# Part of an attention kernel's row maxima taken from one key half and a rectified key difference

## Chip, core and metric

The kernel runs on one core of a Trainium2 chip. The metric is the time of one execution on the device, in microseconds. PE is the matrix engine, DVE the vector engine, ACT the scalar engine, POOL the GpSimd engine, and SP the queue that issues the DMAs.

## The reference

`x` has 8 batches of 1024 tokens of 256 features. One transformer layer, with grouped-query attention and a feed-forward part with ternary weights:

```
h = layernorm(x)
q, k, v = h @ Wq, h @ Wk, h @ Wv          # 16 query heads, 4 key heads, head size 16
q, k = rope(q), rope(k)
p = softmax(q k^T / sqrt(256))            # over the 1024 keys of the batch
x = x + layernorm((p v) @ Wo)
x = x + layernorm(layernorm(x) @ ternary(W)^T * alpha + bias)
```

Everything is float32. Before the exponentials the kernel subtracts each query's largest score, so it computes all scores twice: once with queries on the partitions, to find the maxima, and once with keys on the partitions, for the exponentials and the product with v.

## The kernel before

A *unit* is half a batch, 512 tokens; there are 16. A unit has four *blocks* (one query head of each key head), a block has 8 *steps* (one tile of 128 keys each), so a unit has 32 steps (`SPU`) and the kernel 512. A step has four score tiles of 128 keys by 512 queries.

Queries and keys are stacked in `q_st` and `k_st` as 64 rows a head: the parts high, low, high of q against high, high, low of k (float32 split in two), and two rows that carry the split negative maximum against rows of -1. Two heads share the 128 rows. `q_st` has two buffers (a unit each), `k_st` and `v_aug` (v with a column of ones) have three (a batch each).

The work of PE, DVE and ACT is in the program's order, written by `window()`. A window has three of a block's 32 exp tiles (two in its last). For each, `exp_one` issues one score matmul (L628) into one of three PSUM buffers of one bank and ACT's exponential (L643); behind each, `max_scores` issues one maxima matmul (L576): 128 queries against 512 keys. Two of them (the index `v`, `part = v % 2`) fill a tile `sm` of two banks, with two buffers, and DVE reduces its 1024 columns to one (L590). Then come parts of other stages (`parts_of_step`), and at the end `av_piece` (L663), the product of the exponentials of two windows earlier with v. Maxima run 48 tiles (12 steps) ahead of the exps. When a block's 16 tiles of maxima are done, `shift_split` (L603) splits them, and `shift_rows` transposes them (L610), copies them on ACT (L612) and sends them into `q_st` by two DMAs (L619).

The other stages are put at steps by tables. `P_PARTS` holds a unit's `Project` (layer norm, q, k, v), starting four units' steps early, relative to `SPU * (u - 4)`; `T_PARTS` holds its `Tail` (scaling, Wo, layer norms, feed-forward). For a unit from the third on: `kv_and_dram` makes k and v transposed and sends k to DRAM and back as `k_rot`; `kt` rotates it, splits it (L157, L162) and stores the parts to DRAM (`dk`, L430), and `stack_keys` loads them into `k_st` (L481); `v` transposes v into `v_aug` (L366, L372); `q` and `q_to_dram` (L472) and later `stack_queries` (L542) do the same for q. In the main part POOL's and SP's orders are chosen by a planner with simulated costs. The first units get their keys on the chip (`PickRows`), and the last unit has a tail of its own (`LastTail`), which uses free buffers of `k_st` and `v_aug`.

Of the kernel before, what the change touches and what calls it, by code (L numbers as in the profile page):

```python
# [16 lines left out]
P = 128  # L17
# [3 lines left out]
HD = 16  # L21
UT = 4
UQ = UT * P
EPS = 1e-5
THRESH_FACTOR = 0.7


@with_exitstack
def kernel(
# [103 lines left out]
    k_st, v_aug, q_st = [], [], []  # L133
    for i in range(2):
        q_st.append(const.tile([P, G, 2, UQ], F32R, name=f"q_st{i}"))
    for i in range(3):
        k_st.append(const.tile([P, 2, S], F32R, name=f"k_st{i}"))
        v_aug.append(const.tile([P, NK, HKV, 32], F32, name=f"v_aug{i}"))

# [10 lines left out]
    def fill_constant_parts(i):  # L150
        if i > 0:
            fill_rows(k_st[i], 1, NROW, 64 - NROW)
        nc.gpsimd.memset(v_aug[i], 1.0)

    def split_hi(eng, hi, src):
# [149 lines left out]
    class Project:  # L305
# [54 lines left out]
        def v(self):  # L360

            lo = 0 if self.u < 2 else DK
            pt = psum([P, UT, P], f"ptv_{self.u}")
            for t in range(UT):
                src = self.kv_t[lo:, t * P : (t + 1) * P]
                nc.tensor.transpose(pt[:, t, lo:], src, ident[lo:, lo:])  # L366
            if lo == 0:
                self.k_rot = qkp.tile([P, UT, DK], F32, tag="k_rot", name=f"k_rot_{self.u}")
                nc.scalar.copy(self.k_rot, pt[:, :, :DK])
            if self.u == 0:  # L370
                self.split_q(0, (0,))
            nc.scalar.copy(  # L372
                v_aug[self.b % 3][:, self.half * UT : (self.half + 1) * UT, :, 0:HD],
                pt[:, :, DK:].rearrange("p t (r d) -> p t r d", d=HD),
            )

# [30 lines left out]
        def kv_and_dram(self):  # L407

            u = self.u
            for p in range(2):  # L410
                self.kv(p)
            d_k = dram.tile([DK, UQ], F32, tag="d_k", name=f"d_k_{u}")
            nc.sync.dma_start(out=d_k, in_=self.kv_t[:DK])
            self.k_rot = qkp.tile([P, 2, P], F32, tag="k_rot", name=f"k_rot_{u}")
            src = d_k.rearrange("(m e) (g t) -> e g m t", e=2, t=P)
            for e in range(2):
                nc.sync.dma_start(out=self.k_rot[:, e, :], in_=src[e])

        def kt(self):
            rotate(  # L420
                self.eng, self.k_rot, cos_kt_sb[:, self.half], sin_kt_sb[:, self.half],
                work.tile([P, 2, P], F32, tag="t2k", name=f"t2k_{self.u}", bufs=1),
            )
            hl = qkp.tile([P, 2, 2, P], F32R, tag="k_parts", name=f"ks_{self.u}")
            split(self.eng, hl[:, 0], hl[:, 1], self.k_rot)
            dk = self.dk = dram.tile([2, DK, UQ], F32, tag="dk", name=f"dk_{self.u}")
            dst = dk.rearrange("l (m e) (g t) -> l e g m t", e=2, t=P)
            for l in range(2):
                for e in range(2):
                    nc.sync.dma_start(out=dst[l, e], in_=hl[:, l, e, :].bitcast(F32))  # L430
            self.stack_keys()

        def q_product(self, p):
            if self.q_rot is None:
# [36 lines left out]
                    src = self.hl["q"][64 * c : 64 * (c + 1), l].rearrange("p e t -> p (e t)")  # L471
                    nc.sync.dma_start(out=rows[l, c], in_=src.bitcast(F32))  # L472

        def stack_keys(self):

            keys = slice(self.half * UQ, (self.half + 1) * UQ)
            src = self.dk.rearrange("l (r a d) t -> a l d r t", a=2, d=HD)
            for a in range(2):
                for band, l in enumerate((0, 0, 1)):
                    row = 64 * a + HD * band  # L480
                    nc.sync.dma_start(  # L481
                        out=k_st[self.b % 3][row : row + HD, :, keys].bitcast(F32), in_=src[a, l]
                    )

    def row_pickers():

# [68 lines left out]
            return q_st[u % 2][:, j, r2, :]  # L555
        return q_st[u % 2][:, :, r2, j * P : (j + 1) * P]

    def max_scores(v):


        i, k = divmod(v // 2, 2 * NK)
        u, part = i // G, v % 2
        if i == 0:
            a, ch, t, r2 = 1 - part, k // NK, k // 2 % UT, k % 2
        else:
            a, ch, t, r2 = 1 - k % 2, part, k // 4, k // 2 % 2
        queries = block_queries(i, r2)
        queries = queries[:, t * P : (t + 1) * P] if u < NU - 1 else queries[:, t]
        if part == 0:
            sm[0] = ps_mx.tile([P, 2, 512], F32, tag="sm", name=f"sm_{i}_{k}")  # L570
            if k == 0:
                mx[i] = small.tile([P, 2, UT, 2], F32, tag="mx", name=f"mx_{i}")
            if k == 0 and i == 0:
                mx["half"] = small.tile([P, 2, 2, UT, 2], F32, tag="mx0", name="mx_half", bufs=1)
        rows = slice(64 * a, 64 * a + 64)
        nc.tensor.matmul(  # L576
            sm[0][:, part, :],
            queries[rows],
            k_st[(u // UPB) % 3][rows, r2, ch * 512 : (ch + 1) * 512],
            start=True,  # L580
            stop=True,
        )
        if part == 0:
            return
        if i == 0:
            nc.vector.tensor_reduce(mx["half"][:, ch, ::-1, t, r2], sm[0], AX.X, ALU.max)
            if k == 2 * NK - 1:
                nc.vector.tensor_tensor(mx[0], mx["half"][:, 0], mx["half"][:, 1], ALU.max)
        else:
            nc.vector.tensor_reduce(mx[i][:, a, t, r2 : r2 + 1], sm[0], AX.XY, ALU.max)  # L590
        if k == 2 * NK - 1:
            shift_split(i)
            due.append((v // 4 + (1 if i < 2 else 2), i))

    sm, mhl = {}, {}

    def shift_split(i):

# [7 lines left out]
    def shift_rows(i):  # L606

        hl = mhl.pop(i)
        pm = psum([8 * UT, P], f"pm_{i}", F32R)
        nc.tensor.transpose(pm, hl.rearrange("p a l x -> p (a l x)"), ident_r)  # L610
        mh = work.tile([8 * UT, P], F32, tag="mh", name=f"mh_{i}")
        nc.scalar.copy(mh, pm.bitcast(F32))  # L612
        n = 4 * UT
        for a in range(2):
            row = 64 * a + NROW
            dst = block_queries(i)[row : row + 2].bitcast(F32)
            if len(dst.shape) == 4:
                dst = dst.rearrange("l j c t -> l (j c) t")
            nc.sync.dma_start(out=dst, in_=mh[n * a : n * a + n, :])  # L619


    es, av_ps, av_sb, d_av = {}, {}, {}, {}
# [1 line left out]
    def exp_scores(n, r2, a, sc):  # L624
# [2 lines left out]
        rows = slice(64 * a, 64 * a + 64)  # L627
        nc.tensor.matmul(  # L628
            sc if len(queries.shape) == 2 else sc.rearrange("p (j t) -> p j t", j=G),
            k_st[(i // G // UPB) % 3][rows, r2, kt * P : (kt + 1) * P],  # L630
            queries[rows],
            start=True,
            stop=True,
# [20 lines left out]

    def av_piece(i, first, end):

        va = v_aug[(i // G // UPB) % 3]
# [152 lines left out]
    class LastTail(Tail):  # L810
# [4 lines left out]
        def __init__(self, u):  # L815
            super().__init__(u)
            self.xn = qkp.tile([P, UT, D], F32, tag="xn", name="xn_last", bufs=2)

        def new(self, what, p):
            i = (B - 3) % 3 if what == "x1" else (B - 2) % 3  # L820
            if what == "xn":
                return self.xn[:, p : p + 1]
            if what == "hl":
                tile = k_st[i][:, p // 2, (p % 2) * 2 * D : (p % 2 + 1) * 2 * D]
                return tile.rearrange("p (l t d) -> p l t d", l=2, t=1)
            return v_aug[i][:, 2 * p : 2 * p + 2].rearrange("p t r d -> p (t r d)").unsqueeze(1)

        def eng(self, p):
# [80 lines left out]
    def load(u):  # L909
# [3 lines left out]

    P_PARTS = (
        (26, "begin", 0), (33, "x", 0, 0), (34, "x", 0, 1), (37, "begin", 1), (43, "x", 1, 0),
        (45, "x", 1, 1), (49, "kv_and_dram"), (51, "q", 0), (52, "kt"), (53, "v"), (55, "q", 1),
        (57, "q_to_dram"),
    )
    L_PARTS = (
        (10, "n", 0), (13, "o", 0), (15, "attn", 0), (16, "stats_a", 0), (19, "stats_x", 0),  # L920
# [8 lines left out]
        (29, "x", 1, 1), (31, "ffn", 1), (31, "stats_f", 0), (33, "stats_f", 1),  # L929
    )  # L930

    P_FIRST = (47, 51, 52, 54, 57, 58, 59, 60, 62, 61, 63, 64)
    T_LAST = (1, 3, 4, 5, 9, 10, 11, 14, 17, 20, 21, 21, 22, 24, 25, 26, 23, 27)

    warm = []
# [13 lines left out]
    def third(name, *args):  # L949
        return lambda: getattr(projects[2], name)(*args)  # L950

    for k, fs in enumerate((
        [second("x", 1, 0), second("x", 1, 1), second("kv", 0)],
        [second("kv", 1), (pick, "q", 0, 0, 1), (pick, "q", 0, 1, 1), second("v"),
# [15 lines left out]
        [third("kt")],  # L970
        [],
        [(fill_constant_parts, 2)],
        [],
        [third("q", 0)],
        [],
        [third("q", 1), (stack_queries, 1)],
        [third("q_to_dram")],
    )):
        for f in fs:
# [13 lines left out]
            at(start + k, part, projects, u, *p)  # L993
    for u in range(2, NU):
        at(SPU * (u - 1) + 1, stack_queries, u)
    for u in range(NU - 1):
        start = SPU * (u + 1)
        at(start + 1, begin_tail, u)
# [35 lines left out]

    def start_step(n):
        for _ in range(4):
            max_scores(maxima[0])
            maxima[0] += 1
        parts_of_step(n)

# [11 lines left out]
    def window(i, s, size, late):  # L1052
# [5 lines left out]
        else:  # L1058
            end = min(maxima_by(s + size), 4 * NSTEP)
            for q in range(max(size, end - maxima[0])):  # L1060
                if q < size:
                    exp_one(s + q)
                if maxima[0] < end:
                    max_scores(maxima[0])
                    maxima[0] += 1
        behind.append((i, s, size))
        for n in range(s // 4, (s + size) // 4):
            parts_of_step(n)
# [136 lines left out]
```

## Time and profile before

| | |
|---|---|
| median of 3 runs | 1733.28 us (1733.03 to 1734.47) |
| profiled execution | 1735.28 us, of which span 1733.1 us |
| PE, DVE, ACT, POOL busy | 1602.1, 1398.1, 1271.0, 836.0 us |
| granted PE clock | 0.983 in the mean; 1.00 or near it from about 200 us on |
| DMA | 28.9% of 16 engines' time on the main queue |
| the units from 812 to 1219 us | 407 us for four, PE busy 383.9, DVE 341.3, ACT 312.2 |

Busy time of PE is modelled, since its matmuls overlap. A line of a group gives the source line, engine, operation, written and read tiles with their shapes, the count, then the busy time, the mean duration of one in ns, and the idle time before them with what ended it. Lines such as L590 are of the kernel before. Two lines that occur often are helpers: L157 and L162 are the two steps of a split.

### The profile page before, as it was taken

To read this page: it belongs to the slowest core of one execution; us is meant where nothing else is said; L and a number is where in the kernel's file an instruction comes from. 1 tells how busy PE (TensorE), PEld (TensorE's weight loads), DVE (VectorE), ACT (ScalarE), POOL (GpSimd) and SP (SyncE) were. 2 spreads that over 40 slices of the span, in tenths; PEclk is the share of its full clock that TensorE was granted. 3 is DMA by queue.
4 is the path that set the end of the run, shared out by engine and by line. 5 is a ranking of instruction groups with operands and counts; after the bars stand their busy time and mean duration, and the time that the engine had idled before them with its cause. 6 is when DMAs were issued, how large, how long until landed. Compare 5 with 4: busy or idle time off the path is not lost.

```text
span 1733.1 us, 35758 instructions
## 1 busy us (share of the span) xinstructions
PE 1602.1 (92%) x14200; PEld 834.1 (48%) x14200; DVE 1398.1 (81%) x1752; ACT 1271.0 (73%) x2479; POOL 836.0 (48%) x1239
## 2 busy tenths in 40 slices
PE   7969999999999999999999999999999999999997
PEld 5534454444544445454454544545454544444444
DVE  6848778888788888878888788888978887888874
ACT  4637777777687777868777777877777786877775
POOL 5522447274453637346374644737455362333354
PEclk8879999999999999999999999999999999999999
DMA  4330424225151332515124151412414141140100
GB/s 131 66 78 32 83 73 87 63 76 97 41 101 43 82 82 61 104 39 98 51 74 96 54 102 46 90 58 78 84 48 95 45 87 51 33 82 32 40 14 25
DMA packets 86071, 117.88 MB, mean 68 GB/s; under 512 B 12089, under 2 KB 50809, under 8 KB 85753
## 3 DMA queue, kind: packets, MB, share of 16 engines
q1 hardware_dynamic: 85904, 115.60, 28.9%
q8 instruction: 112, 1.84, 0.5%
q14 instruction: 55, 0.44, 0.1%
HBM read 68.65 MB, written 45.88 MB: 66 GB/s over the span
## 4 chain that ended last, share of the span: by engine, by line
PE 34%; DVE 13%; POOL 4%; ACT 4%; issue 1%; DMA 1%; SPq 0%; POOLq 0%; ACTq 0%; DVEq 0%
PE av L663 13%; DVE mx L590 10%; PE se L628 10%; PE sm L576 4%; ACT e L643 3%; PE pa L283 2%; PE pf L283 1%; PE pq L283 1%; PE pt_ot L267 1%; DMA dq<-hlq 1%; DVE bnst L237 1%; PE pkv L283 1%; PE pt_xt L267 1%; POOL hlq L162 1%; DVE mhl L603 0%
## 5 line engine op out<-in xcount | busy, mean ns | idle before, releaser
L590 DVE TENSOR_REDUCE mx<-sm 128x1 f32<-128x1024 f32 x1008 | 1190.5, 1218 | 285.5 <-PE sm L576 242.2
L643 ACT ACTIVATE e<-se 128x512 f32<-128x512 f32 x2000 | 1055.9, 602 | 301.3 <-PE sm L576 238.5
L576 PE MATMUL sm<-k_st,q_st 64*128 64x512 f32 x2048 | 736.2, 449 | 45.7 <-DVE mx L590 41.8
L628 PE MATMUL se<-q_st,k_st 64*128 64x512 f32 x2048 | 685.8, 434 | 19.3 <-DMA q_st<-mh 18.3
L663 PE MATMUL av<-e,v_aug 128*32 128x256 f32 (+3 forms) x8096 | 591.7, 392 | 0.0
L628 PEld LDWEIGHTS se<-q_st,k_st 64*128 64x128 f32 x2048 | 330.8, 186 | 368.3 <-ACT e L643 217.3
L576 PEld LDWEIGHTS sm<-k_st,q_st 64*128 64x128 f32 x2048 | 324.5, 186 | 156.7 <-DVE mx L590 125.0
L663 PEld LDWEIGHTS av<-e,v_aug 128*32 128x32 f32 x8096 | 184.3, 109 | 192.6 <-issue 145.7
L241 POOL TENSOR_SCALAR lnsc<-mv 128x2 f32<-128x2 f32 (+1 forms) x134 | 25.8, 193 | 453.6 <-DVE mv L239 448.7
L737 POOL TENSOR_TENSOR xn<-xn,a 128x512 f32<-128x512 f32 x30 | 38.4, 1280 | 129.0 <-DMA a<-d_rec 115.1
L798 POOL TENSOR_TENSOR a<-a,bias_bc 128x512 f32<-128x512 f32 x30 | 39.0, 1300 | 117.2 <-ACT a L797 117.2
L242 POOL TENSOR_TENSOR lnsc<-lnsc,mhalf 128x2 f32<-128x2 f32 (+1 forms) x134 | 92.9, 694 | 0.9
L162 POOL TENSOR_TENSOR hl<-xn,hl 128x512 fp32r<-128x512 f32 x60 | 76.4, 1285 | 0.5
L253 POOL TENSOR_SCALAR xn<-x,lnsc 128x256 f32<-128x256 f32 x116 | 64.9, 568 | 3.4
L297 POOL TENSOR_TENSOR t<-q_rot,sin_q_sb 128x512 f32<-128x512 f32 x31 | 39.7, 1282 | 32.1 <-ACT q_rot L439 32.1
L764 ACT COPY a<-pa 128x512 f32<-128x512 f32 x30 | 17.6, 586 | 45.6 <-issue 45.6
L283 PE MATMUL pq<-xt,wqkvh 128*128 128x256 f32 x256 | 46.1, 304 | 2.8 <-ACT e L643 2.8
L237 DVE BATCH_NORM_STATS2 bnst<-a 128x6 f32<-128x256 f32 x120 | 44.6, 413 | 4.7 <-POOL a L798 4.7
L283 PE MATMUL pa<-woh,hl 128*128 128x256 f32 x240 | 47.0, 298 | 0.2 <-ACT e L643 0.2
L237 DVE BATCH_NORM_STATS2 bnst<-x 128x6 f32<-128x256 f32 x124 | 45.9, 412 | 1.1 <-DMA x<-in_L_attn_x 1.1
L267 PE MATMUL pt_xt<-ident_r,xs 128*128 128x128 f32 x256 | 33.4, 260 | 12.7 <-ACT e L643 11.1
L283 PEld LDWEIGHTS pq<-xt,wqkvh 128*128 128x128 f32 x256 | 36.3, 197 | 14.6 <-ACT e L643 13.2
(156 smaller groups left out, 1320.0 us busy)
## 6 DMA issues: line engine op xcount, KB each, us to landing
q_st<-dq SPq DMA_DIRECT2D x90, 256.0 KB
dq<-hlq SPq DMA_DIRECT2D x60, 256.0 KB
d_av<-avsb SPq DMA_DIRECT2D x60, 256.0 KB
x<-in_L_attn_x SPq DMA_DIRECT2D x15, 512.0 KB
xn<-d_av SPq DMA_DIRECT2D x30, 256.0 KB
a<-d_rec SPq DMA_DIRECT2D x30, 256.0 KB
xr<-in_L_attn_x SPq DMA_DIRECT2D x15, 512.0 KB
out_x<-a SPq DMA_DIRECT2D x30, 256.0 KB
```

Of the source, the lines that this page charges most:

```text
L162: eng.tensor_tensor(lo, src, hi.bitcast(F32), ALU.subtract)
L237: nc.vector.bn_stats(st[:, t, :], src[:, t, :])
L242: nc.gpsimd.tensor_tensor(sc[:, 1, :], sc[:, 1, :], mhalf[:, :n], ALU.pow)
L253: eng.tensor_scalar(dst[:, t, :], src[:, t, :], sc[:, 0, t : t + 1] if eng is nc.gpsimd else mv[:, t, 0:1], sc[:, 1, t : t + 1], ALU.add i ...
L267: nc.tensor.transpose(pt[:, c, t * P : (t + 1) * P], src[:, t, c * P : (c + 1) * P], ident_r)
L283: nc.tensor.matmul(out, chunk(left[i], c), chunk(right[j], c), start=(k == 0), stop=(k == len(steps) - 1),)
L297: eng.tensor_tensor(dst, x, table.unsqueeze(1).to_broadcast(list(x.shape)), ALU.mult)
L576: nc.tensor.matmul(sm[0][:, part, :], queries[rows], k_st[(u // UPB) % 3][rows, r2, ch * 512 : (ch + 1) * 512], start=True, stop=True,)
L590: nc.vector.tensor_reduce(mx[i][:, a, t, r2 : r2 + 1], sm[0], AX.XY, ALU.max)
L628: nc.tensor.matmul(sc if len(queries.shape) == 2 else sc.rearrange("p (j t) -> p j t", j=G), k_st[(i // G // UPB) % 3][rows, r2, kt * P : ...
L643: nc.scalar.activation(e, sc, AF.Exp, scale=1.0 / D**0.5)
L663: nc.tensor.matmul(av_ps[0][32 * r : 32 * r + 32, lo:hi], va[:, kt, r, :], es[i * NK + kt, r // 2, r % 2][:, lo:hi], start=(kt == 0 and lo ...
```

## The change

For part of the tiles the maximum over the two key halves is taken as max(s1 + max(s2 - s1, 0)), column by column, where s1 are the scores of the first 512 keys and s2 - s1 are scores of key differences.

- A new buffer `k_df` holds, for a batch, the second half's keys less the first half's, split and stacked as keys are. `k_differences` computes them on POOL from the two units' `k_rot` (which gets a second buffer), `k_to_dram` splits and stores them, and `stack_differences` loads them.
- In `max_scores`, when a window ends between the two matmuls of a tile (`v + 1 == end`), the tile's first matmul takes `k_df` and its second the first key half. After the window's exps `positive_differences` has ACT write the positive part of the first bank to an SBUF tile `rest`; after the second matmul, DVE's `tensor_tensor_reduce` adds the second bank to `rest` and takes the largest. The other tiles are reduced as before. Blocks of the first batch, and the first block of each later one, have no such tile.
- `k_st` and `v_aug` have two buffers in place of three. `v` and `stack_keys` move to later steps, the start's third unit too. The last tail keeps its `x1` in a buffer of `x`.

```diff
+    k_df = const.tile([P, 2, S // 2], F32R, name="k_df")
-    for i in range(3):
+    for i in range(2):
         k_st.append(const.tile([P, 2, S], F32R, name=f"k_st{i}"))
         v_aug.append(const.tile([P, NK, HKV, 32], F32, name=f"v_aug{i}"))
...
             fill_rows(k_st[i], 1, NROW, 64 - NROW)
+            fill_rows(k_df, 1, NROW, 64 - NROW)
...
-            dk = self.dk = dram.tile([2, DK, UQ], F32, tag="dk", name=f"dk_{self.u}")
+            self.dk = self.k_to_dram("dk", self.k_rot)
+
+        def k_to_dram(self, tag, k):
+
+            hl = qkp.tile([P, 2, 2, P], F32R, tag="k_parts", name=f"{tag}s_{self.u}")
+            split(self.eng, hl[:, 0], hl[:, 1], k)
+            dk = dram.tile([2, DK, UQ], F32, tag=tag, name=f"{tag}_{self.u}")
             dst = dk.rearrange("l (m e) (g t) -> l e g m t", e=2, t=P)
             for l in range(2):
                 for e in range(2):
                     nc.sync.dma_start(out=dst[l, e], in_=hl[:, l, e, :].bitcast(F32))
-            self.stack_keys()
+            return dk
+
+        def k_differences(self):
+
+            first = projects[self.u - 1].k_rot
+            self.eng.tensor_tensor(first, self.k_rot, first, ALU.subtract)
+            self.dkd = self.k_to_dram("dkd", first)
...
+        keys = k_st[(u // UPB) % 2][:, :, ch * 512 : (ch + 1) * 512]
         if part == 0:
...
+            sm["rest"] = None
+            if v + 1 == end and u >= UPB and i % (UPB * G) > 0:
+                sm["rest"] = work.tile([P, 512], F32, tag="rest", name=f"rest_{i}_{k}")
+                keys = k_df
+        elif sm["rest"] is not None:
+            keys = k_st[(u // UPB) % 2][:, :, :512]
...
-            k_st[(u // UPB) % 3][rows, r2, ch * 512 : (ch + 1) * 512],
+            keys[rows, r2],
...
+        elif sm["rest"] is not None:
+            rest, m = sm["rest"], mx[i][:, a, t, r2 : r2 + 1]
+            nc.vector.tensor_tensor_reduce(
+                rest, sm[0][:, 1, :], rest, 1.0, LEAST, ALU.add, ALU.max, m
+            )
...
+    def positive_differences(v):
+        if v % 2 and sm["rest"] is not None:
+            nc.scalar.activation(sm["rest"], sm[0][:, 0, :], AF.Relu)
...
-        (45, "x", 1, 1), (49, "kv_and_dram"), (51, "q", 0), (52, "kt"), (53, "v"), (55, "q", 1),
-        (57, "q_to_dram"),
+        (45, "x", 1, 1), (49, "kv_and_dram"), (51, "q", 0), (52, "kt"), (55, "q", 1),
+        (57, "q_to_dram"), (67, "v"), (68, "stack_keys"),
...
+    at(8 - START + 10, third("stack_keys"))
+    for u in range(3, NU, UPB):
+        at(SPU * (u - 4) + (66 if u == 3 else 55), part, projects, u, "k_differences")
+        at(SPU * (u - 1) - 11, part, projects, u, "stack_differences")
...
                 if maxima[0] < end:
-                    max_scores(maxima[0])
+                    max_scores(maxima[0], end)
                     maxima[0] += 1
+            positive_differences(maxima[0])
```

The shift rows' DMAs are kept in `shifts`, and `behind_shift` queues the third unit's `kt` and the second unit's `stack_queries` on SP behind those of block 1.

More of the change, by code (lines that the diff above doesn't have):

```diff
@@ L25 @@
 THRESH_FACTOR = 0.7
+LEAST = -3.4e38
 @with_exitstack
@@ L367, in v @@
             if lo == 0:
-                self.k_rot = qkp.tile([P, UT, DK], F32, tag="k_rot", name=f"k_rot_{self.u}")
+                self.k_rot = qkp.tile([P, UT, DK], F32, tag="k_rot", name=f"k_rot_{self.u}", bufs=2)
                 nc.scalar.copy(self.k_rot, pt[:, :, :DK])
@@ L372, in v @@
             nc.scalar.copy(
-                v_aug[self.b % 3][:, self.half * UT : (self.half + 1) * UT, :, 0:HD],
+                v_aug[self.b % 2][:, self.half * UT : (self.half + 1) * UT, :, 0:HD],
                 pt[:, :, DK:].rearrange("p t (r d) -> p t r d", d=HD),
@@ L413, in kv_and_dram @@
             nc.sync.dma_start(out=d_k, in_=self.kv_t[:DK])
-            self.k_rot = qkp.tile([P, 2, P], F32, tag="k_rot", name=f"k_rot_{u}")
+            self.k_rot = qkp.tile([P, 2, P], F32, tag="k_rot", name=f"k_rot_{u}", bufs=2)
             src = d_k.rearrange("(m e) (g t) -> e g m t", e=2, t=P)
@@ L423, in kt @@
             )
-            hl = qkp.tile([P, 2, 2, P], F32R, tag="k_parts", name=f"ks_{self.u}")
-            split(self.eng, hl[:, 0], hl[:, 1], self.k_rot)
-            dk = self.dk = dram.tile([2, DK, UQ], F32, tag="dk", name=f"dk_{self.u}")
+            self.dk = self.k_to_dram("dk", self.k_rot)
[3 more added lines that the diff above has]
+            dk = dram.tile([2, DK, UQ], F32, tag=tag, name=f"{tag}_{self.u}")
             dst = dk.rearrange("l (m e) (g t) -> l e g m t", e=2, t=P)
@@ L472, in q_to_dram, with stack @@
                     nc.sync.dma_start(out=rows[l, c], in_=src.bitcast(F32))
-        def stack_keys(self):
-            keys = slice(self.half * UQ, (self.half + 1) * UQ)
-            src = self.dk.rearrange("l (r a d) t -> a l d r t", a=2, d=HD)
+        def stack(self, dst, dk):
+            src = dk.rearrange("l (r a d) t -> a l d r t", a=2, d=HD)
             for a in range(2):
@@ L480, in stack_keys, with stack_differences @@
                     row = 64 * a + HD * band
-                    nc.sync.dma_start(
-                        out=k_st[self.b % 3][row : row + HD, :, keys].bitcast(F32), in_=src[a, l]
-                    )
+                    nc.sync.dma_start(out=dst[row : row + HD].bitcast(F32), in_=src[a, l])
+        def stack_keys(self):
+            keys = slice(self.half * UQ, (self.half + 1) * UQ)
+            self.stack(k_st[self.b % 2][:, :, keys], self.dk)
+        def stack_differences(self):
+            self.stack(k_df, self.dkd)
     def row_pickers():
@@ L556, in block_queries, with max_scores @@
         return q_st[u % 2][:, :, r2, j * P : (j + 1) * P]
-    def max_scores(v):
+    def max_scores(v, end):
         i, k = divmod(v // 2, 2 * NK)
@@ L593, in max_scores @@
             due.append((v // 4 + (1 if i < 2 else 2), i))
-    sm, mhl = {}, {}
+    def positive_differences(v):
+        if v % 2 and sm["rest"] is not None:
+            nc.scalar.activation(sm["rest"], sm[0][:, 0, :], AF.Relu)
+    sm, mhl, shifts = {}, {}, {}
     def shift_split(i):
@@ L618, in shift_rows @@
                 dst = dst.rearrange("l j c t -> l (j c) t")
-            nc.sync.dma_start(out=dst, in_=mh[n * a : n * a + n, :])
+            shifts[i] = nc.sync.dma_start(out=dst, in_=mh[n * a : n * a + n, :]).ins
     es, av_ps, av_sb, d_av = {}, {}, {}, {}
@@ L629, in exp_scores @@
             sc if len(queries.shape) == 2 else sc.rearrange("p (j t) -> p j t", j=G),
-            k_st[(i // G // UPB) % 3][rows, r2, kt * P : (kt + 1) * P],
+            k_st[(i // G // UPB) % 2][rows, r2, kt * P : (kt + 1) * P],
             queries[rows],
@@ L655, in av_piece @@
     def av_piece(i, first, end):
-        va = v_aug[(i // G // UPB) % 3]
+        va = v_aug[(i // G // UPB) % 2]
         if first == 0:
@@ L817, in __init__ @@
             self.xn = qkp.tile([P, UT, D], F32, tag="xn", name="xn_last", bufs=2)
+            self.x1s = xp.tile([P, UT, D], F32, tag="x", name="x1_last", bufs=2)
         def new(self, what, p):
-            i = (B - 3) % 3 if what == "x1" else (B - 2) % 3
+            i = (B - 2) % 2
             if what == "xn":
@@ L825, in new @@
                 return tile.rearrange("p (l t d) -> p l t d", l=2, t=1)
+            if what == "x1":
+                return self.x1s[:, p : p + 1]
             return v_aug[i][:, 2 * p : 2 * p + 2].rearrange("p t r d -> p (t r d)").unsqueeze(1)
@@ L930 @@
     )
-    P_FIRST = (47, 51, 52, 54, 57, 58, 59, 60, 62, 61, 63, 64)
+    P_FIRST = (47, 51, 52, 54, 57, 58, 59, 60, 62, 63, 64, 61, 65)
     T_LAST = (1, 3, 4, 5, 9, 10, 11, 14, 17, 20, 21, 21, 22, 24, 25, 26, 23, 27)
@@ L950, in third, with behind_shift @@
         return lambda: getattr(projects[2], name)(*args)
+    def behind_shift(i, f, *args):
+        with tc.issue_after(shifts[i]):
+            f(*args)
     for k, fs in enumerate((
@@ L969 @@
         [third("v"), second("split_q", 1), second("q_to_dram")],
-        [third("kt")],
         [],
-        [(fill_constant_parts, 2)],
+        [],
+        [],
         [],
         [third("q", 0)],
-        [],
-        [third("q", 1), (stack_queries, 1)],
+        [(behind_shift, 1, third("kt"))],
+        [third("q", 1), (behind_shift, 1, stack_queries, 1)],
         [third("q_to_dram")],
@@ L1036, in start_step @@
         for _ in range(4):
-            max_scores(maxima[0])
+            max_scores(maxima[0], None)
             maxima[0] += 1
@@ L1063, in window @@
                 if maxima[0] < end:
-                    max_scores(maxima[0])
+                    max_scores(maxima[0], end)
                     maxima[0] += 1
+            positive_differences(maxima[0])
         behind.append((i, s, size))
```

## Prediction

> **What bounds the kernel now.** I read the page first: busy shares, then the chain, then the costliest groups.
>
> ```profile
> PE 1602.1 (92%) x14200; PEld 834.1 (48%) x14200; DVE 1398.1 (81%) x1752; ACT 1271.0 (73%) x2479; POOL 836.0 (48%) x1239
> ...
> PE 34%; DVE 13%; POOL 4%; ACT 4%; issue 1%; DMA 1%; SPq 0%; POOLq 0%; ACTq 0%; DVEq 0%
> PE av L663 13%; DVE mx L590 10%; PE se L628 10%; PE sm L576 4%; ACT e L643 3%; PE pa L283 2%; PE pf L283 1%; PE pq L283 1%; PE pt_ot L267 1%; DMA dq<-hlq 1%; DVE bnst L237 1%; PE pkv L283 1%; PE pt_xt L267 1%; POOL hlq L162 1%; DVE mhl L603 0%
> ...
> L590 DVE TENSOR_REDUCE mx<-sm 128x1 f32<-128x1024 f32 x1008 | 1190.5, 1218 | 285.5 <-PE sm L576 242.2
> L643 ACT ACTIVATE e<-se 128x512 f32<-128x512 f32 x2000 | 1055.9, 602 | 301.3 <-PE sm L576 238.5
> L576 PE MATMUL sm<-k_st,q_st 64*128 64x512 f32 x2048 | 736.2, 449 | 45.7 <-DVE mx L590 41.8
> ```
>
> PE looks full, yet the chain (it covers 57% of the span) spends 10% in the maxima's reduction: PE waits for DVE on the way. The waits, longest first, say who waits for whom; a weight load's wait there partly hides under running matmuls.
>
> ```profile
> DVE mx L590 <- PE sm L576: 242.2, 339, 14.0
> ACT e L643 <- PE sm L576: 238.5, 406, 2.0
> PEld se L628 <- ACT e L643: 217.3, 460, 0.7
> PEld sm L576 <- DVE mx L590: 125.0, 204, 2.3
> PE sm L576 <- DVE mx L590: 41.8, 119, 1.8
> ```
>
> DVE waits for PE and PE for DVE: a loop of latencies, not one full engine. The timeline of 837 to 845 us shows it (start, duration, what; then idle time before).
>
> ```profile
> 837.79 0.60 ACT L676 COPY avsb<-av 128x512 f32<-128x512 f32 x1
> 838.26 1.62 ACT L643 ACTIVATE e<-se 128x512 f32<-128x512 f32 x3
> 840.53 3.25 ACT L643 ACTIVATE e<-se 128x512 f32<-128x512 f32 x6 [0.65 <-PE sm L576]
> ...
> 840.57 3.49 DVE L590 TENSOR_REDUCE mx<-sm 128x1 f32<-128x1024 f32 x3 [0.70 <-PE sm L576]
> 844.76 1.23 DVE L590 TENSOR_REDUCE mx<-sm 128x1 f32<-128x1024 f32 x1 [0.70 <-PE sm L576]
> ...
> 841.68 0.49 PE L628 MATMUL se<-q_st,k_st 64*128 64x512 f32 x1
> 842.41 0.39 PE L628 MATMUL se<-q_st,k_st 64*128 64x512 f32 x1
> 842.98 0.50 PE L576 MATMUL sm<-k_st,q_st 64*128 64x512 f32 x1 [0.17 <-DVE mx L590]
> 844.19 0.50 PE L628 MATMUL se<-q_st,k_st 64*128 64x512 f32 x1
> ```
>
> Call a window of three exps *open* when its third maxima matmul fills only the first half of a tile, and the next one *closing*. In the open window at 841.68 that matmul starts 0.57 us behind the exp matmul at 842.41 which it normally accompanies: it needs the bank pair whose reduction ends at about 842.9. The loop is: release 0.06, last matmul and AV 1.21 (842.98 to 844.19), second half landed 0.57 (to 844.76), two reductions 2.4, together 4.2 us for a pair of windows that PE alone does in 3.35 (the fastest take 1.68 each). Sorting all starts between 200 and 1420 us in this way: the score groups of 238 open windows lose 105 us against their fastest form (102 lose nothing, 83 over 0.8 us) and those of 238 closing windows 58 us.
>
> **The change, part by part.** Counting the windows' ends: 5 of a block's 16 tiles are open at a window's end; batches 1 to 7 have 7 blocks each that may use it, so 245 tiles.
>
> *Off DVE, onto ACT.* The two-operand op reads 512 in place of 1024 elements. No row shows it. Near ones, in the lines' own views:
>
> ```profile
> L271 DVE CAST ot<-pt_ot x2: 671/682/692, 1689.1 to 1707.2; 128x512 fp32r<-128x512 f32 x2
> ...
> L162 DVE TENSOR_TENSOR xs<-xn,xs x3: 680/681/1777, 9.1 to 26.2; 128x512 fp32r<-128x512 f32 x3
> ```
>
> Both give 0.68 for 512 elements. The third xs row took 1.78 while POOL worked: with that mixed in evenly the op would cost 1.2 us and nothing would be saved. The Trainium skill, SBUF — State Buffer, "Who interferes with whom", says that a DVE instruction with at most one SBUF input, outside the two-port modes, does not contend with GpSimd; this op has one input in PSUM. By the rule it is 0.68 plus the accumulator. For that the VectorE: DVE Perf Modes page ("Two Vector instructions with no wait between them") counts a second instruction, without a price; no run here shows one. Bounds 0.68 to 1.22; I take 0.75, near the undisturbed rows. DVE loses 245 x 0.47 = 115 us of work. ACT gains 245 rectifications at the exps' 0.60, 0.49 of it uncovered when back to back (three in 1.57): 120 us.
>
> *When the result comes.* The rectification stands behind the window's three exps. In the waiting pair above (open window at 837.36) the third exp ends at 839.88, so it runs until about 840.4, inside ACT's 0.65 us gap, and the second half lands at 840.57: the op gives 0.47 back. Behind an open window that did not wait (860.95) six exps run without a gap; the rectification would end near 863.6 where the old reduction started at 863.19, so op and reduction end together: nothing won. Done for all 245 tiles with everything else left in place: the op starts 0.15 later in the mean and releases 0.32 earlier; the wait of the third matmul that uses the following tile's bank again exists behind 132 of them. The smaller of wait and gain, tile by tile, sums to 35 us (41 at 0.70, 25 at 0.85, 15 at 1.00, 0 at 1.22). But an open window that stops waiting becomes the early kind, behind which the next one wins nothing; I keep two thirds: -24, and -4 for first matmuls that wait for the tile itself (0.17 at 841.85 us).
>
> *What ACT delays.* 118 of the 245 rectifications push the next ACT instruction, 33 us in all, 0.28 each. Behind them wait that window's exps, and the exp matmuls that need their three banks. Most of it lands in windows that wait for DVE anyway. Between 0 and 33; I take +6.
>
> *The second group on other keys.* Same matmuls, same shapes: 0. Its cover is that different banks of the tile are read and written; if the tile were guarded as a whole, see the rivals.
>
> *Key differences.* Once a batch POOL adds 0.73 + 0.41 + 0.73 = 1.9 us, 13 us in all, in 48% busy POOL; without that cover up to 13. I take +1. Ten more DMAs a batch (four dk and six k_st now take 2.34 and 3.55 us of SP's queue): 70, on engines 29% busy. The stacking waits for the last reading of the old differences; behind it on SP stand the shift rows, for which PE now waits 18 us in eight cases. Between -5 and +15; I take +2.
>
> *Moved and dropped.* V's transposes and its ACT copy move 14 steps later in the project and pass the q product; the four dk stores stay with k, the six k_st loads move 16 steps later, behind that q store. They are needed half a unit (51 us) later. Two key buffers for three: the overwritten batch ended 3 steps (9 us) before. The tail's tiles move to a free x buffer. At the start the fill count is unchanged, unit 2's keys go behind a shift row. All 0, bounds -3 to +5: cover is that slack.
>
> Sum: -24 - 4 + 6 + 1 + 2 = -19 us against the profiled execution's own 1735.3 (span 1733.1), which lies 2.0 above the median: 1716.3 there, 1714 as a median.
>
> **Rivals.**
> - *ACT becomes the limit (slower).* A pair then needs 7 x 0.49 = 3.43 us of ACT, over PE's 3.35, before any of the copies, some 0.6 each (837.79). For: six exps already run without gap for 3.25 us. Against: ACT is 73% busy and idle 0.65 to 0.94 us in waiting pairs. It decides once the op starts more than 0.5 us later than the reduction did. With all 33 us of push on PE, and 5 to 10 won, plus queues 3: +28 on the median, 1761. Chance 0.25, with slower ends to 1780.
> - *The tile is guarded as a whole.* Then the change doesn't overlap its halves: the closing window's first matmul waits about 0.9 us for the rectification, 245 times: about 1950. The profile has no such tile. 0.03.
> - *The relay ties.* The op at about 1.0 us or always late: 15 x 2/3 - 9 = 1 us won, 1732. 0.10.
> - *The waits dissolve.* The static 41 us hold in full, pushes vanish in waits, and closing windows win 15 of their 58: 1677; 0.17.
> - The forecast, 1700 to 1727: 0.45.
>
> **How the numbers follow.** About 0.2% (3.5 us) is what a measurement can tell from no change. Faster 0.45 + 0.17 + 0.04 of the tie = 0.66; same 0.04; slower 0.25 + 0.03 + 0.02 = 0.30. Range 1674 to 1758: it takes in the dissolving case, and half of the slower one; the likeliest case alone is 1700 to 1727.
>
> **What would show it.** Right: 245 two-operand rows of 0.70 to 0.80 us, 763 reductions left, DVE busy near 1283, ACT near 1391; L576's wait for DVE (41.8) down by a third or more; exp matmuls' waits for ACT up little. Wrong: rows of 1 us or over; DVE's wait for the rectification ending most of its idle time; PE idle behind ACT's exps by 20 us or more; SP stalls of several us ahead of shift rows.

## The result and the profile after

The changed kernel takes 1780.6 us (median of 4 runs, 1776.8 to 1785.9) against 1733.2 before: 1.0274 times as long (95% interval 1.0245 to 1.0303), 47 us slower. The prediction said 1714, with 1674 to 1758 as its range. The profiled execution took 1778.75 us, its span 1777.0, at a mean granted clock of 0.988 (before 0.983), so the clock is not the cause.

The page of the changed kernel: busy shares, shares of the chain by engine, and the groups that the change touches. Its line numbers are shifted: the maxima matmul L576 is now L602, the reduction L590 is L621, the exponential L643 is L678, and the exp matmul L628 is L663. The number L628 now stands for the new rectification, and L617 for the new two-operand operation.

```profile
PE 1635.8 (92%) x14200; PEld 843.9 (47%) x14200; DVE 1272.2 (72%) x1997; ACT 1391.9 (78%) x2724; POOL 846.1 (48%) x1259
...
PE 52%; ACT 28%; DVE 8%; POOL 4%; DMA 4%; issue 3%; SPq 1%; ACTq 0%; POOLq 0%
...
L621 DVE TENSOR_REDUCE mx<-sm 128x1 f32<-128x1024 f32 x763 | 916.4, 1219 | 167.7 <-PE sm L602 137.2
L602 PE MATMUL sm<-k_st,q_st 64*128 64x512 f32 x1803 | 578.6, 454 | 72.9 <-ACT rest L628 64.8
L617 DVE CUSTOM_DVE_ANT_0 rest<-sm,rest 128x512 f32<-128x512 f32 x245 | 169.5, 692 | 285.9 <-PE sm L602 281.1
L628 ACT ACTIVATE rest<-sm 128x512 f32<-128x512 f32 x245 | 153.5, 626 | 0.9 <-PE sm L602 0.9
```

The work moved just as the prediction counted it: 245 two-operand operations, 763 reductions left, DVE busy 1272 (predicted 1283), ACT busy 1392 (predicted 1391). PE issues the same 14200 matmuls as before and yet is "busy" 34 us longer: the ends of its matmuls are modelled, so a longer busy time is not more work. The new thing stands in the line of L602: most of the maxima matmul's idle time is ended by ACT's rectification. DVE is less in demand, but the two-operand operation sits behind 286 us of idle time that PE ends.

The waits of the changed kernel (us in total, times, longest):

```profile
DVE rest L617 <- PE sm L602: 281.1, 240, 2.5
PEld se L663 <- ACT e L678: 247.0, 555, 0.8
...
DVE mx L621 <- PE sm L602: 137.2, 173, 4.9
...
PEld sm L602 <- ACT rest L628: 122.0, 183, 0.8
PE sm L602 <- ACT rest L628: 64.8, 178, 0.5
...
PE sm L602 <- DVE mx L621: 13.9, 35, 1.3
```

The wait for DVE that the change was to shorten fell from 41.8 to 13.9 us. In its place are two lines in which the maxima matmul and its weight load wait for the rectification. These matmuls write a bank that no rectification reads. The timeline of one pair of windows, PE, ACT and DVE in turn (start, duration, what, idle time before it):

```profile
861.35 0.39 PE L602 MATMUL sm<-k_df,q_st 64*128 64x512 f32 x1
...
862.46 0.50 PE L663 MATMUL se<-q_st,k_st 64*128 64x512 f32 x1
863.43 0.50 PE L602 MATMUL sm<-k_st,q_st 64*128 64x512 f32 x2 [0.47 <-ACT rest L628]
863.76 0.39 PE L663 MATMUL se<-q_st,k_st 64*128 64x512 f32 x1
...
861.31 1.58 ACT L678 ACTIVATE e<-se 128x512 f32<-128x512 f32 x3 [0.63 <-PE sm L602]
862.76 0.62 ACT L628 ACTIVATE rest<-sm 128x512 f32<-128x512 f32 x1
...
864.25 1.09 ACT L678 ACTIVATE e<-se 128x512 f32<-128x512 f32 x2 [0.38 <-PE sm L602]
...
863.96 0.69 DVE L617 CUSTOM_DVE_ANT_0 rest<-sm,rest 128x512 f32<-128x512 f32 x1 [1.16 <-PE sm L602]
864.58 0.08 DVE L617 DVE_READ_ACCUMULATOR2_ANT mx<- 128x1 f32 x1
```

The open window's key-difference matmul starts at 861.35. Its rectification stands on ACT behind three exps and runs from 862.76 to 863.38. The closing window starts its exp matmul at 862.46, but the maxima matmul beside it starts at 863.43, 0.05 behind the rectification's end and 0.97 us late. PE's order is fixed, so the next exp matmul is late too (863.76), and then ACT (0.38 us before 864.25) and DVE (1.16 before 863.96) wait.

### The profile page after: what moved, and what is told of

The parts are those of the page before. It is cut to its first block, busy times and chain, and to the rows that moved or that the text cites. A ratio compares the mean times of both kernels' runs of the same rounds, so it can differ in the third digit from the quotient of the medians.

```text
span 1777.0 us, 36663 instructions
## 1 busy us (share of the span) xinstructions
PE 1635.8 (92%) x14200; PEld 843.9 (47%) x14200; DVE 1272.2 (72%) x1997; ACT 1391.9 (78%) x2724; POOL 846.1 (48%) x1259
## 4 chain that ended last, share of the span: by engine, by line
PE 52%; ACT 28%; DVE 8%; POOL 4%; DMA 4%; issue 3%; SPq 1%; ACTq 0%; POOLq 0%
ACT e L678 21%; PE av L698 17%; PE se L663 15%; PE sm L602 9%; ACT rest L628 5%; DVE mx L621 4%; PE pa L286 3%; PE pq L286 2%; PE pf L286 2%; PE pkv L286 1%; ACT avsb L711 1%; PE pt_xt L270 1%; DVE rest L617 1%; PE pt_ot L270 1%; DVE mhl L638 1%
## 5 line engine op out<-in xcount | busy, mean ns | idle before, releaser
L678 ACT ACTIVATE e<-se 128x512 f32<-128x512 f32 x2000 | 1082.1, 604 | 254.6 <-PE sm L602 206.4
L621 DVE TENSOR_REDUCE mx<-sm 128x1 f32<-128x1024 f32 x763 | 916.4, 1219 | 167.7 <-PE sm L602 137.2
L663 PE MATMUL se<-q_st,k_st 64*128 64x512 f32 x2048 | 704.3, 434 | 9.9 <-DMA q_st<-mh 8.8
L602 PE MATMUL sm<-k_st,q_st 64*128 64x512 f32 x1803 | 578.6, 454 | 72.9 <-ACT rest L628 64.8
L663 PEld LDWEIGHTS se<-q_st,k_st 64*128 64x128 f32 x2048 | 342.3, 186 | 378.6 <-ACT e L678 247.0
L617 DVE CUSTOM_DVE_ANT_0 rest<-sm,rest 128x512 f32<-128x512 f32 x245 | 169.5, 692 | 285.9 <-PE sm L602 281.1
L602 PEld LDWEIGHTS sm<-k_st,q_st 64*128 64x128 f32 x1803 | 244.8, 187 | 158.6 <-ACT rest L628 122.0
L628 ACT ACTIVATE rest<-sm 128x512 f32<-128x512 f32 x245 | 153.5, 626 | 0.9 <-PE sm L602 0.9
L602 PE MATMUL sm<-k_df,q_st 64*128 64x512 f32 x245 | 112.2, 458 | 9.2 <-DVE mx L621 7.4
L602 PEld LDWEIGHTS sm<-k_df,q_st 64*128 64x128 f32 x245 | 45.0, 184 | 47.4 <-DVE mx L621 40.2
```

The costliest lines, as they stand in the source:

```text
L602: nc.tensor.matmul(sm[0][:, part, :], queries[rows], keys[rows, r2], start=True, stop=True,)
L617: nc.vector.tensor_tensor_reduce(rest, sm[0][:, 1, :], rest, 1.0, LEAST, ALU.add, ALU.max, m)
L628: nc.scalar.activation(sm["rest"], sm[0][:, 0, :], AF.Relu)
L663: nc.tensor.matmul(sc if len(queries.shape) == 2 else sc.rearrange("p (j t) -> p j t", j=G), k_st[(i // G // UPB) % 2][rows, r2, kt * P : ...
L678: nc.scalar.activation(e, sc, AF.Exp, scale=1.0 / D**0.5)
```

## Experiments

Three theories stood after this reading. *The guard* (G in the expectations): the program makes the tile's second matmul wait until ACT has read the first bank. *ACT's load* (rival A): 245 more ACT instructions delay the exps whatever the matmul waits for; the chain spends 28% on ACT now, 4% before. *The rest of the change* (rival S): moved steps, two key buffers and more DMAs. The times below are medians. The kernel before ran beside the experiments, on one chip at 1734.8 us (experiments 1 to 4) and on another at 1733.6 us (5 to 8).

**1. The change without the guard.** Declares that the second matmul does not depend on the rectification. The rectification of the other bank, and DVE's operation behind both, stay as they are.

```diff
-        nc.tensor.matmul(
+        mm = nc.tensor.matmul(
             sm[0][:, part, :],
...
+        if sm["rest"] is not None:
+            tc.declare_no_dep(mm.ins, sm["relu"], reason="other bank")
...
-            nc.scalar.activation(sm["rest"], sm[0][:, 0, :], AF.Relu)
+            sm["relu"] = nc.scalar.activation(sm["rest"], sm[0][:, 0, :], AF.Relu).ins
```

> The changed kernel, but the second matmul of each of the 245 split tiles is declared independent of the rectification of the first half, which reads another PSUM bank. Theory G (the wait of that matmul for the rectification is the cost): in the changed kernel the score groups of closing windows lose 144 us against 58 before, those of open windows 69 against 105; without the wait the closing windows go back to about 58 and the 35 us of the open ones stay won: 1700 to 1725 us. Rival A (ACT's queue is the cost: 245 rectifications push the exps): still over 1760 us, with PE's waits for ACT's exps in place of those for the rectification. Rival S (moved steps, two key buffers, more DMAs are the cost): still over 1760 us, with no wait on ACT to see.

Measured: 1704.9 us, 0.982 of the kernel before (0.978 to 0.986). That is 76 us less than the changed kernel (beside whose runs the kernel before took 1.7 us less) and 30 less than the kernel before. Its waits, where the line numbers behind L602 are two higher:

```profile
PEld se L665 <- ACT e L680: 259.1, 595, 0.9
ACT e L680 <- PE sm L602: 159.7, 298, 6.0
DVE mx L623 <- PE sm L602: 156.6, 206, 5.1
...
DVE rest L619 <- PE sm L602: 96.9, 82, 4.0
...
DVE rest L619 <- ACT rest L630: 77.0, 127, 1.0
...
PE sm L602 <- DVE mx L623: 30.2, 43, 2.2
```

No line has a maxima matmul waiting for the rectification any more; DVE's operation waits for it, as the change meant, up to 1.0 us at a time. A pair in this kernel's timeline:

```profile
917.31 0.50 PE L602 MATMUL sm<-k_df,q_st 64*128 64x512 f32 x1
...
918.53 0.50 PE L665 MATMUL se<-q_st,k_st 64*128 64x512 f32 x1
918.53 0.82 PE L602 MATMUL sm<-k_st,q_st 64*128 64x512 f32 x2
...
918.66 0.62 ACT L630 ACTIVATE rest<-sm 128x512 f32<-128x512 f32 x1
919.13 1.61 ACT L680 ACTIVATE e<-se 128x512 f32<-128x512 f32 x3
...
919.30 0.69 DVE L619 CUSTOM_DVE_ANT_0 rest<-sm,rest 128x512 f32<-128x512 f32 x1 [0.51 <-ACT rest L630]
```

The closing window's first exp matmul and its first maxima matmul both start at 918.53, before the rectification of the other bank has even begun (918.66), and the operation starts 0.02 behind the rectification's end.

**2. The moves only.** No split tile at all; key differences, buffers, queue order and moved steps of the change stay.

```diff
-            if v + 1 == end and u >= UPB and i % (UPB * G) > 0:
+            if False:
```

> The changed kernel with no split tile: all maxima by the old reduction, no rectification; the key differences, their DMAs, two key buffers and the moved steps stay. G: 1730 to 1740 us, as before. A: the same. S: 1765 us or more.

Measured: 1721.4 us, 0.992 (0.990 to 0.995). Rival S falls. Theory G's range missed too: it had the moves at nothing or a small loss, and they win 12 to 13 us. Experiment 5 looks for that. So the split itself is worth 1704.9 - 1721.4 = -16.5 us without the guard, and about 1780.6 - 1721.4 = +59 with it.

**3. The guard with the old reduction.** Plain keys in every tile and the full 1024-column reduction; the rectification stays between the two matmuls of the 245 tiles, and its result is not used.

```diff
-                keys = k_df
-        elif sm["rest"] is not None:
-            keys = k_st[(u // UPB) % 2][:, :, :512]
...
-        elif sm["rest"] is not None:
-            rest, m = sm["rest"], mx[i][:, a, t, r2 : r2 + 1]
-            nc.vector.tensor_tensor_reduce(
-                rest, sm[0][:, 1, :], rest, 1.0, LEAST, ALU.add, ALU.max, m
-            )
```

> The changed kernel, but both halves of the split tiles are plain scores, reduced in full by DVE as before; the rectification still reads the first bank ahead of the second matmul and its result is unused. So it has the wait and ACT's load and not the shorter DVE work. G: slower than the changed kernel by what DVE's shorter work had won there, some 35 us: 1800 to 1830 us. A: the same as the changed kernel or little above. S: 1780 us.

Measured: 1805.5 us, 1.041 (1.037 to 1.045). The waits for the rectification (here L620) are there without any new DVE operation:

```profile
PEld sm L599 <- ACT rest L620: 82.8, 130, 0.8
...
PE sm L599 <- ACT rest L620: 39.5, 85, 0.5
```

**4. ACT's load with the old reduction.** As 3, but ACT rectifies the window's first exp tile, in SBUF, into the unused tile: one more ACT instruction of the same size at the same place, which no matmul waits for.

```diff
-    def positive_differences(v):
+    def positive_differences(v, s):
         if v % 2 and sm["rest"] is not None:
-            nc.scalar.activation(sm["rest"], sm[0][:, 0, :], AF.Relu)
+            n, (a, r2) = s // 4, divmod(s % 4, 2)
+            nc.scalar.activation(sm["rest"], es[n, r2, a], AF.Relu)
...
-            positive_differences(maxima[0])
+            positive_differences(maxima[0], s)
```

> All maxima by the old reduction; behind the exps of the same 245 windows ACT rectifies an exponential tile in SBUF (the window's first, 128x512) into the unused tile: ACT's load at the same place of its queue, with no tie to the maxima. G: 1735 to 1750 us (pushes of 33 us at most, mostly hidden). A: 1765 us or more. S: like the run with moves only.

Measured: 1723.1 us, 0.993 (0.991 to 0.995), 1.6 us above experiment 2, which is within the spread of both. ACT is busy nearly as long here as in the changed kernel (1392):

```profile
PE 1605.9 (93%) x14200; PEld 835.1 (49%) x14200; DVE 1403.3 (82%) x1752; ACT 1378.9 (80%) x2724; POOL 848.2 (49%) x1259
```

So rival A falls: ACT's load alone costs next to nothing. (G's range, 1735 to 1750, missed by the same 12 us of the moves.) Experiments 3 and 4 differ in what the rectification reads and in what waits for it: 1805.5 - 1723.1 = 82 us. With the short DVE operation (changed kernel and experiment 1) the same difference is 76.

**5. Where the moves win.** Experiment 2 without the new order on SP at the start: the key transfers of the third unit and the query transfers of the second are queued as they come ready, not behind block 1's shift rows (blocks and units count from 0).

```diff
-        [(behind_shift, 1, third("kt"))],
-        [third("q", 1), (behind_shift, 1, stack_queries, 1)],
+        [third("kt")],
+        [third("q", 1), (stack_queries, 1)],
```

> The run with moves only, but the third unit's key part and the second unit's query loads are not queued behind block 1's shift rows on SP. The run with moves only was 12 us faster than the kernel before, and its trace is 13 us ahead at block 1's first exp and about the same from there on. Theory Q (SP's queue at the start: the shift rows of block 1 stood behind these transfers): that 13 us comes back, 1730 to 1737 us. Rival (the moved v and key steps or the buffers bring it): stays at 1718 to 1725 us.

Measured: 1738.1 us (12 runs), 1.0022 (1.0004 to 1.0040), which is 16.7 us above experiment 2 (that one on the other chip). PE's wait for the shift rows is one line in each kernel; in order, the kernel before, experiment 2, experiment 5:

```profile
PE se L628 <- DMA q_st<-mh: 18.3, 8, 13.0
```

```profile
PE se L663 <- DMA q_st<-mh: 6.0, 2, 5.4
```

```profile
PE se L663 <- DMA q_st<-mh: 19.8, 5, 12.2
```

In the kernel before and in experiment 5 the longest of them is at the start of block 1. SP's queue there, in the same order of kernels:

```profile
90.07 3.30 SPq L481 DMA_DIRECT2D k_st<-dk  x6
93.42 2.30 SPq L542 DMA_DIRECT2D q_st<-dq  x5
96.23 1.41 SPq L619 DMA_DIRECT2D q_st<-mh  x2
```

```profile
87.28 1.40 SPq L654 DMA_DIRECT2D q_st<-mh  x2
88.77 2.35 SPq L437 DMA_DIRECT2D dk<-dks  x4
91.17 2.86 SPq L559 DMA_DIRECT2D q_st<-dq  x6
```

```profile
84.16 2.62 SPq L437 DMA_DIRECT2D dk<-dks  x4
88.29 2.21 SPq L559 DMA_DIRECT2D q_st<-dq  x5
90.55 7.94 SPq L493 DMA_DIRECT2D k_st<-dk  x6
100.79 2.28 SPq L654 DMA_DIRECT2D q_st<-mh  x2
```

ACT's copy of these rows starts at about 87 us in all three. Behind the key loads they leave at 96.2 (before) and 100.8 (experiment 5), with the new order at 87.3. Block 1's first exp matmul starts at 105.85 us in the kernel before, at 92.59 in experiment 2 and at 104.38 in experiment 5. So about 12 of the 16.7 us stand at this one place; the rest was not traced, and experiment 5 ran on another chip.

The other moves, and the key differences' 70 extra DMAs, then cost 1738.1 - 1733.6 = 4.5 us (0.7 to 7). One new stall of that size shows, at the start of block 5, in every kernel with the moves. There the loads of the key differences stand ahead of the shift rows; in experiment 2 (SP, then PE):

```profile
197.38 5.28 SPq L493 DMA_DIRECT2D k_df<-dkd  x6
202.75 1.39 SPq L654 DMA_DIRECT2D q_st<-mh  x2
...
204.83 0.76 PE L663 MATMUL se<-q_st,k_st 64*128 64x512 f32 x1 [5.44 <-DMA q_st<-mh]
```

**6 and 7. Do all 245 split tiles pay?** The open windows at exp tiles 0 and 24 of a block hardly waited even before the change (table below). Both kernels start from experiment 1. In 6, the rectification of those two windows is issued ahead of the window's third exp, so that DVE's operation can start sooner. In 7 those two tiles are not split, which leaves 147.

```diff
-        nc.scalar.activation(e, sc, AF.Exp, scale=1.0 / D**0.5)
+        return lambda: nc.scalar.activation(e, sc, AF.Exp, scale=1.0 / D**0.5)
...
-                if q < size:
-                    exp_one(s + q)
+                exp = exp_one(s + q) if q < size else None
+                held = q == 2 and exp is not None and s % (4 * NK) in (0, 24)
+                if exp is not None and not held:
+                    exp()
...
-            positive_differences(maxima[0])
+                if held:
+                    positive_differences(maxima[0])
+                    exp()
+            if not held:
+                positive_differences(maxima[0])
```

```diff
-            if v + 1 == end and u >= UPB and i % (UPB * G) > 0:
+            if v + 1 == end and u >= UPB and i % (UPB * G) > 0 and k not in (5, 9):
```

> The run without the guard, and in the windows at 0 and 24 of a block, whose third maxima matmul doesn't wait, ACT rectifies ahead of the window's third exp in place of behind it. Theory L (behind a window that did not wait the rectification comes so late that the shorter DVE operation wins nothing): the open windows at 6, which lose 0.77 us to the reduction's bank, lose 0.3 to 0.5 us; with 49 such and some loss for the later exp, 1685 to 1702 us. Rival (order on ACT does not matter, the loop is set elsewhere): 1700 to 1710 us. Rival A (a later exp holds PE up as much): 1705 to 1720 us.

> The run without the guard, with the split tiles only at the windows at 6, 12 and 18 of a block (147 tiles); those at 0 and 24 are reduced in full. L: the two left out won nothing, so the same time within 4 us of the run without the guard (1701 to 1709 us). If every tile's shorter DVE work counts alike: 7 us slower, 1711 us. If ACT's load counts: faster, under 1700 us.

Measured: 6 takes 1716.7 us, 0.989 (0.987 to 0.991); 7 takes 1704.3 us on the same chip, 0.984 (0.980 to 0.988), the same as experiment 1. So 6 missed theory L's range by about 15 us, and 7 met it: the two tiles a block that were left out had won nothing, and pulling their rectification forward loses. The table below shows how: the window at 6 loses 0.53 in place of 0.77 us, as hoped, but those at 3 and 27 lose 0.45 in place of about 0.22. That fits rival A's account for this place, that a third exp pushed back holds its PSUM buffer, and so PE, in the next window; the exp matmuls' weight loads, which waited 259.1 us for ACT in experiment 1, wait longer:

```profile
PEld se L665 <- ACT e L680: 285.7, 680, 0.8
```

**8. The rectification ahead of the third exp in every open window.** Experiment 6 with `held` for every `s`.

> The run without the guard, with the rectification ahead of the window's third exp everywhere. L: in windows whose third maxima matmul waits, ACT then waits for it with the exp behind; their successors stall: slower than with the early place in free windows alone, 1695 to 1715 us. Rival A: over 1715 us.

Measured: 1714.4 us, 0.988 (0.986 to 0.991). It lies in the range that was given, but is not above experiment 6 as was said; the two are alike. Experiments 1 and 7 are the best of all kernels and no different from each other; no run beat them.

**Where the loss sits.** For each window, the time from its first exp matmul to the first matmul of other work behind its group of exp and maxima matmuls, less the shortest such time (0.89 us); the mean in us by the window's first exp tile within the block, between 300 and 1420 us of each profile:

| | 0 open | 3 clos. | 6 open | 9 clos. | 12 open | 15 clos. | 18 open | 21 clos. | 24 open | 27 clos. |
|---|---|---|---|---|---|---|---|---|---|---|
| before | .08 | .20 | .82 | .17 | .42 | .30 | .79 | .30 | .10 | .26 |
| after | .08 | .83 | .60 | .37 | .16 | .67 | .51 | .45 | .09 | .82 |
| 1, no guard | .07 | .22 | .77 | .16 | .26 | .44 | .72 | .37 | .05 | .23 |
| 6, early in two | .07 | .45 | .53 | .17 | .27 | .44 | .66 | .38 | .05 | .45 |

The guard hits the closing windows at 3 and 27 most (+0.6 us), where the open windows ahead of them hardly waited; at 9, 15 and 21 it adds 0.1 to 0.25 over experiment 1.

The same losses summed from block 8 on, the first of batch 1 (273 open and 272 closing windows), in us:

| | open | closing | both |
|---|---|---|---|
| before | 131 | 64 | 195 |
| 2, moves only | 132 | 65 | 196 |
| after | 80 | 176 | 256 |
| 1, no guard | 105 | 74 | 179 |
| 3, guard, full reduction | 136 | 144 | 279 |
| 4, ACT's load only | 127 | 73 | 199 |

These sums account for the measured times: against the moves only, the change loses 60 (measured 59) and experiment 1 wins 17 (16.5); 3 lies 80 above 4 (82).

## Why the prediction was wrong

**The step that failed** is "*The second group on other keys.* Same matmuls, same shapes: 0. Its cover is that different banks of the tile are read and written". In the source the two matmuls and the rectification do name different halves of `sm`, and experiment 1 shows that the overlap works. The program that runs does not use it: it orders PE's second matmul behind ACT's read of the same tile. The case was a rival, "The tile is guarded as a whole", at a chance of 0.03. "The profile has no such tile" was its only argument, and that means unknown, not excluded. The guard costs 76 to 82 us (after against 1, 3 against 4). Against the moves alone the split then loses 59 us where it was to win 22, and 59 less the moves' 12 is the 47 measured. Whether the program orders every use of two halves of a tile in this way, no run here shows.

**The rival's price was wrong as well.** It said 0.9 us times 245, about 220 us, hence 1950. The single pair at 863.43 does lose 0.97. Over the closing windows of the split tiles the matmul starts 0.9 us behind the window's first exp matmul at 3 and 27, 0.8 at 15, and 0.4 at 9 and 21, where ACT is done at about the time that the window begins: 0.67 in the mean, or 164 us for 245. The windows' loss grows by less, 102 us over experiment 1 (74 to 176), for some were late without the guard too (0.44 and 0.37 at 15 and 21). And 25 us come back in the open windows (105 to 80), which leaves 77. With the full reduction nothing comes back: open windows lose 127 us in experiment 4 and 136 in 3.

**The gain's mechanism was there, and smaller.** Open windows lose 51 us less in the changed kernel (131 to 80), which looks like more than the forecast gain. But half of it comes only with the guard: in experiment 1 they lose 105. Without the guard the split is worth -16.5 us in all, where the prediction had -24 - 4 + 6 = -22. In experiment 1 the gain sits mostly in the open windows at 12 (0.42 to 0.26), and the closing windows at 15 and 21 give part back (0.30 to 0.44 and 0.37). The remark that nothing is won behind an open window that did not wait is right: experiment 7 leaves those 98 tiles whole and loses nothing. The price of ACT's pushes, +6 from bounds of 0 to 33, measured +1.6 beside full reductions (4 against 2).

**The unknown operation** was taken at 0.75 us and measured 0.69:

```profile
L617 DVE CUSTOM_DVE_ANT_0 rest<-sm,rest x245: 690/692/695, 273.5 to 1719.1; 128x512 f32<-128x512 f32 x123
L617 DVE DVE_READ_ACCUMULATOR2_ANT mx<- x245: 82/83/84, 274.1 to 1719.7; 128x1 f32 x123
```

The least, median and most of 245 lie within 5 ns, though 131 of them ran beside an instruction of POOL. So the upper bound of 1.22, from the xs row of 1.78, did not apply, and the Trainium skill's rule (SBUF — State Buffer, "Who interferes with whom") held where the trace had been ambiguous. The second instruction takes 0.083 us, and the next operation starts 0.62 behind the first one's start, so it costs nothing to speak of.

**Moved and dropped** were all put at 0, with bounds of -3 to +5, "unit 2's keys go behind a shift row" among them. The new order at the start, unit 2's keys and unit 1's queries behind the shift rows, is worth -16.7 us (2 against 5). The sign was in the trace of before: SP's shift rows stood behind the key loads, and one of PE's eight waits for them took 13.0 us. The prediction used that line only as a sum of 18 us, for a loss that the key differences might bring. That loss came too, the 5.4 us at block 5: the rest of the moves and the key differences came to +4.5, against the +3 that the prediction gave to the key differences.

Put together: without the guard the change gives 1704.9, 9 us below the forecast, since the moves won some 15 us more than foreseen and the split 5.5 less. That this lies within 1700 to 1727 is in part luck: the moves' gain was not in the sum. The guard puts 76 on top.

**ACT as the limit**, the slower rival with 0.25, looks right in the changed kernel's chain (28% ACT, exps at its head) and is wrong. ACT is busy 1373 us in experiment 1, which is faster than before, and 1379 in experiment 4, which is no slower than 2. In the changed kernel the chain runs through ACT because a matmul waits for the rectification, which is queued behind exps.

**The signs named in advance did not tell.** All but one of the signs of being right came true in the slower kernel (the operation's rows were 0.69 us, not 0.70 to 0.80), and of the signs of being wrong only the stall on SP. L576's wait for DVE fell by two thirds in the slower kernel (41.8 to 13.9) and by only 28% in the faster one of experiment 1 (to 30.2). The exp weight loads' wait for ACT, 217 before, rose to 247 in the slower kernel and to 259 in the faster one. The one line that told is a releaser that did not exist before: "PE sm L602 <- ACT rest L628".

## What to carry to other kernels

When a change makes one engine write a part of a buffer while another reads a different part, ask what the program's waits are kept on, the part or the whole tile, and price the whole-tile case before trusting the overlap; in the profile it shows as a new releaser of the writer. Price the guarded case by where it falls: here it cost 0.6 us in each window that ran nearly on time without it and had to wait 0.9 for ACT, and 0.1 to 0.25 in the others. And look at single long waits in a group's line (8 times, 18.3 us, longest 13.0): the order of a queue can be worth as much as the change itself.

## What was not expected of the hardware

PE writing one bank of a tile while ACT reads the other has hardly a price. In experiment 1, 213 of the 245 rectifications overlap a maxima matmul; they take 634 ns in the mean and 617 in the median, against 626 and 618 in the changed kernel, where none does. So the overlap that the guard forbids is one that these runs show to be cheap.
